# PSUM places of a recurrence given out by use, and its second state p kept at another scale

## The chip, the cores and the metric

The kernel runs on one core of a Trainium2 chip. Its engines are TensorE (PE in the profile; PEld is its weight load), VectorE (DVE), ScalarE (ACT), GpSimd (POOL) and SyncE (SP, which issues DMAs). The metric is the device time of one execution in microseconds (us). Times before are the median of three runs; the profile is of one execution.

## The reference

The input `x` has 128 sequences of 32 steps with 256 features; `cond` is one vector of 256 for each sequence. Two layers follow each other, and each adds its result to `x`.

Layer 0 runs a recurrence over the 32 steps for all 128 sequences, with states q and p that both begin as `cond`. A step is one fourth-order Runge-Kutta step (h = 0.01) of

```
dq = q - q**3 / 3 - p + x[:, t] + tanh(q) @ coupling.T + bias
dp = 0.08 * (q + 0.7 - 0.8 * p)
```

and then clips q and p to +-20. The states q of all steps go through a gated feed-forward net, 256 to 1024 to 256, whose activations and weights are quantized in blocks of 32.

Layer 1 normalizes, scales and shifts by `cond`, runs attention with 16 heads over the 32 steps of a sequence, and then a feed-forward net of the same size with Hadamard rotations, 8-bit activations and ternary weights.

## The kernel before

All arithmetic of the recurrence is in float32 tiles of 128 partitions by 256 columns. q, its stage values q2, q3 and m4, and their tanh are kept with the 256 features as two chunks of 128 partitions and the 128 sequences as columns in each chunk.

**Phase one** has the recurrence, `step(t, q, p, d)`, and behind it, for each t, the first feed-forward net and the way to the second layer's normalized input, `ffn0(t, q)`. **Phase two** has the second layer in 32 tiles of 128 tokens, `tokens(g)`. Most PSUM tiles of phase one are given up before phase two begins.

**One step.** A stage of Runge-Kutta has `slope(i, qi)`: ACT's tanh (L890) and square (L891, into PSUM); PE's coupling matmuls (L897), which add onto the stage's PSUM tile `ps[i]`; and DVE's cube (L904), which multiplies square plus constant by the stage value. DVE's `nest` (L831), a multiply and add, then makes the next stage value from `ps[i]` and the cube. So the four stages are one chain: nest, tanh, matmuls, nest. Its end is the clipped sum `add_sat` (L949) that gives the next q.

p is held negated and shifted, and z, the p of the next step, is built in p's own place by three nests and an `add_sat` (also L949). In a step p is read

- by ACT (L907), which copies it into `ps[0]` as the start of the first stage's sum;
- by DVE, in the nests that start `ps[1]`, x and z;
- by ACT (L915), which writes `part`, p at the scale of w. POOL (L917) adds q to it to give w, which ACT later brings into `ps[3]` (L933).

x is a partial sum that DVE makes early in the step and reads for `ps[2]`.

**PSUM.** A bank holds 512 float32 columns, so two places of 256. The tiles named `ps_sum` are two banks with four places. Three of them, `ps_sum` 0, 1 and 2, are one pool for z/p, x and the squares: whichever is free is taken. The fourth, `shared`, lies beside place 2 and holds small constants and scratch of the quantization: `floor`, `none` and `power` (single columns that DVE reads as bounds in the clips, L1242, and in the block scales, L993 and L1000) and `ps_tiny`. `ps[0]` and `ps[2]` are one bank (`ps_stage0`), `ps[1]` and `ps[3]` another.

**Order.** Every piece of work is recorded by `add(engine, cost, fn, reads, writes, ...)`. `Work.order` puts the pieces of each phase on the engines one by one: it keeps for each engine the earliest start, from estimated costs, dependences and free places, and breaks ties by a due time for each piece. The due times are the two strings of `TIMES`, two characters for each piece. Before a longer planned gap on PE, `keep_warm` puts matmuls of zeros (L1717). The engines then run their instructions in that order, each with waits on semaphores.

The planner knows, of PSUM banks, that a DVE instruction after DVE's own write to the same bank starts later. It has no term for two engines on one bank.

Of the kernel before, what the change touches and what calls it, by code (L numbers as in the profile page):

```python
# [25 lines left out]
ALPHA = 0.7  # L26
# [79 lines left out]
class Work:  # L106
# [15 lines left out]
            "4s6R5d4Q4A3T5X4f6d656I5v6T6B5o1_003P360_3i2A474y5l3N2L473a535E4B4n7M6E6X7i7J6m7w9IArBy5y6g6j6s6b5x84"  # L122
            "6A8w95B8CMBs6a5W745s6p6d8oAUB7BwB6C6CB9d736U9a9e7c8iBRCNCBCrEMC_AO7s8p9t9K9BAYCKC6DOEGEkFfAg8G8qAhAV"
            "9EBsCiDZEFEjEnFH7I7uAY82Em6J8s7s8Y8r9NH78c8x8P7A8H9bAS9SAw808W878c8G8G9b8mBwAZCIBK5H6u74686K4b6j2V5u"
            "3G6M736F2l4y4k5A5O6R6s7h5x6K5D5V6f5t738K6A8I7c7n706p6-647t8m8j795x7P7n8W979j97AcAUA-BBCIE9CxDpEzD2DE"
            "CaEpE9EcF2FRF8FcFjFQF_GAGJ6gGkGsGXGjGWGfGpH8GdHNHGHUHEJ07o5x6-8Q7_7Y8Y7k7d80816T84AJ7t7D7W809t7o7d9R"
            "7C7r8a9M8L8h9hAI9A999b9K8kAfAP9r8c949WAgAt9W9vAkAvBZC7CuD6E9DBFTFnCYExDSEqFVFyG5G4FsGMGHGBGVGaGgHQHK"
            "HiHbJaHfHUI4HpHXIVIQJJJJKvA87V7wANAg9TBe9cB5C68Z9W9WAG9q9EAVBOApAA9sC89fB8AhBWBnA7C9BmBSAkAZAUAWBgBP"
            "A5BCBYAs7jBhB4BsBEBaBRC2DVDYFbDrG4GeD8FJE9F5FbG7G_H9HFHuHmGzHdHYJPIUIvIuIxKSIrJ0J9J6IyJkJUMXN2OhCpA5"
            "CXB9BSBYAkBPBYCvBCBDBmBvBHCiCECTBMBpBxBaAVBzCbCeC3BxCVD8C6C4BuCNBzCgCxCXBZCQC67zDgChCPCLD4CeDeCQELGK"  # L130
            "EwHVI2FvFVFkFTGoHEIEIFHbITIdI8IyIZK5JSJpJ_K3L3JuKTKBKfJuKpLgM-OiRfBDC1CmDrBcB-D4CMDNDbEDCDDGDGCMCADO"
            "DZDwCUCaClBvClCtDCCbCaDGDyD4CPDKCCBcDRDmCRDBDFD78ND8CMDyDtGIGxH1GtIBI1HhIeIhI1IPHuIEHzIoJ0J9J1JVJUJU"
            "JkK2KxLjLZLiMQMZMFMIMbN2MqLhN5OpQbTME9DGECEVC_CoCVDSDcEFEBCwDfECDeDtDYDeDsE4DbDXDaDWDfDwE1E3DvETDyE0"
            "E8DyEKEOE9EQEUE5ETJBF9G-H7IEICIRI0JiJ2J0J2JdJrJEJPJDJLK3J-K9KrMCLHMMMALbLjOGNSMFLzNDQpN5MLNwLmN9MmOg"
            "PRQQQqEuDSDvETEbF5F8EyEcEnExFAEeEuFNFSF4F4FPFbFWFXFbFjFKFPFOFxFLFSFnFiFzFuFzFgFmF-G6G6GFJoI7J7JEJGJQ"
            "JNJRKbLbM5MeNAN9LRKJLsMHMhLsMcM5NcMZMuN4M-M_RKOuOFN4OaR0OWNaOUOePCOqPAQEQUReELEaEzFlG1GLGTGdF-G1GIGU"
            "FnG8GlGaGGGHGtGsGmGyGuGtGeGgH5H6GmGgHBHHHMH0HCH7HBHKHZHPHgKvIPJHJiJzK1KIMINwMFMSMwNQNCMTMuOZO5N-NbN1"
            "NSNHNVNLMzOKNGUGPpOfPQQdR2PwPvRCPNQTQ7QrRUSNS8G1FtGCH9HZHyH-H-HOHSHxI0HAHeI9I9HkHpI8IIIEIKIJIMHsIBIC"
            "IbIGIGIaIhIdILIiISIaIjIsInI-POJoJxMVMWOENBNaPENoObPOP6OKOTOgPCPmOQPWP9PdPFP3PQPyPSQjS7QZQYQRRmQSSIQA"
            "RzPQRnRGSVTLUZT4GqHSHcIWIrJ6I_J5IwImJCJAIcJ6JFJNJAJJJnJdJRJeJSJqJcJhJyJ-JkJnK2K7KCJvJ-K7KBKIKDK3K9No"  # L140
            "NZNIOQNuONNqN2T8P6PSQ7PxQMOyPiQgQNOXQIQrQUQ3QbQtPVQmPaQkSURBT1SyR_TMPrUMQxTsSlUKUUUvTMIvIfJ6K8KvKYLQ"
            "LDK-L8KlKkKiLoL0LELzMIKwLcLvLaLpLiLtL_LpLnLiMPLkL_LWM9M0MLMeLRMEL-M1QCPIP-PeP2O_PSPjQzQnR5RFRsS2QhRZ"
            "RkSmPkSSRgS5QoSpRKRQSeRMSIUdTgTMUdRBUUTvVCSgUdUaVcVxW2UeKjKxMhMPLmMKLzL_MSMcL_MHLoMJMgMkNFNOMHMRMLMl"
            "MNMgNqNcNGNDNvNxN7NRNCMCMpOEOUNVNQN4NMTEQYQIQdQzQuR7Q9RISwT8TYStSuT9TKUJUcT7TESUTFTfUPSxTVTjT9RLUPUq"
            "V5WPUOVsVyWEV_WAX4XHXQYWWmNDMQNhO4NKNkNoNlO2OnNmNHOaNUO7NIOiOuNoNRNqO3NxOZOeOfNnNvPGOvOGOHOUNmOZOiP3"
            "OjP4OZOXQoRRQ-RrRvSJSZRnSEU0UHVDUYUGU_UxVJVoVYUPUZUJWjVYWsVYVNVQTRVhWJXBXhWjWxWMY1YoXtY4XtY-YsYxRVNy"
            "ObPRO4PEP5P5PCPQNyOWPQPsO_PePePkOaPQPYPGP9PqQFQJP8PnQKQQPYPgPpPTQ3QMQoPrPTPQQBRaTMU1TSTDTdTeUJUGVFVO"
            "V3VqW4VgVjW8WRX8W0WcVtXrWPXfYcW7XfVrXlYJYSY8a2XqYXZ2avYSZPZGaubkc8RTQ1PxQNPpPmPnQ7QMQqPvQBQYO2QgQLQ_"
            "RFQZQrQEQZR5QYRdRcR2RFRtSLRPRcRAQwRmRFRqRqR3QmRUTDTMTeTfT2UBUXSxT1WDXCWqWpWwW6W9XmWkZBXWYJXvXyXwZLYQ"
            "XpaHZ4ZkYjYmZVbRZWXLZrYKZvZVaHbKcUcxQhQfQ-S8RKRaS4R_S4S7RgRWSKPkRyRiSNSQS8RQRYSISHSETUTXSKRsTqTiSYSO"  # L150
            "SRSlSiTUT_T0S1SYSTU6U-UZVHU-V6VGWNVsXRXsYhZ9YVYLYqXfXuZZYPYeZ2YQYZXzaAZDYycPaFZpaVaHc3auaib9bma7ahay"
            "e5d8fBRbRoSSTaRoSaTKSUTbTtTHSXUNRRTESKTsUhTCTQTNTLSwSWUNUgU8TWVEUkTGSlUGTXTQVBVCTzTlTLUhU3W4W8VyX8Wp"
            "WgYlYMYCZUZ0bCZIYza9a5YUXiZwZpZgY8aAYfZbaGb3bXb_c3bNbgbvbEbXbudUbXcvcIeseXexRwTxTsUeU8TnUsToUjU7UVTv"
            "VcUBUQTtVkVeV4UyU7VLU9UyVLWMUZUvVvVPV9W9VhV1VqWKWtVSV2VEWCYEYTXcXXXwXhYSY_YdZhamZaaOb2aTb9aHaCZfaoaM"
            "ataab1dCahc8dDdVcUcpddcaeod8dldSeidYeYeRfQfKdvR-V8VmW0UWVrVrV-W5WUVdVmWbXLVBW3W6WBW7VhVtWJVlVuVhXRW-"
            "WQWMXdVsWxX1WbXNVzVwWrWJXJWzbfaaavZha_a9aRamcRanaxbmbyc2bKc7cFb_e4cycJcod0dadJdldSdseeelfLeJekfFfwed"
            "f5fgewfsf3gwgAibSGVrWrWqXLWyXqWyXBXFX2XLXDYoXSWoXLXOZ8XxXvXCXUXoXdXjXSYoY8YSY3YOYzYgYAXNXnYlXbXwXtbh"
            "bJbAarb4aqb9eLducedkcydOd7dWd9dMd9eKdkeUd-die4fUcleCfRf3fiewfEfOgcfVg4fqfdf9gFghhzhmi8VmWLXdYGYRXwYJ"
            "YPYEYTXiYUX-XFYiZaZiZ4Y-Z7YOYvYQYCYGZ7ZeZYZKZLa5Z8YrYKYcZea2YmZ2YRZkdhb3bbcUcUcgcCeMd7e7ewdpfRfWeaf3"
            "ejfwfgfHfDfGgZf1g1fIgLfrfjgagUhAhZh5hWiShLiGgmiIinjIiSl6ZQXAYZZWZMZxa2a1ZbZzZ9Z-ZXZ8ZyZ5ZjaUaDZMaoZQ"  # L160
            "ZYZLaFaOZwa6ambDZmZ_alaHanaTapaBaaZzbTbbcXdddDcedIdMeGeTf-gOfcfpgQgNgbg4fMfxgthCgei2f-hch4hEhzifili2"
            "hOiSjhiTh9iHhCi_jkipkejol4Z9a1aBbNaEanb9b9a_b1aibEamcRakbQb4bIbmbDbOcAc8c4bObocGcQbpcEc8cicccObTbdbj"
            "dMczcHc9e9eYedeGfCeef9eif6gihZg7h7hhgMhJgChGiYgqh1h6hzhPiYi1hkiZjyikkBkNjQk8jVj9jmkbjwkjkQnlodpFbpaj"
            "bDcWd3ccdEcvbhcQcYd9cFcpcmcscUcxc-c_dCd_crdldEdJe5dteBdceEeJeie1e1dvePeGeSdSefgDh5g3ffftgIg9hFh1hQjE"
            "hNiPiui9hxhyiCiqioijixh_jQiqj9jAiDkzkikvkEkdo5kZjokUkbkol3lCpspbs8cWcCcOdoeYedeae5eHeef1eaeieAeceJe3"
            "eyf3e_egf2fdfPeNfGenf0f6fIf2fhfcebeTfGfZfcfEeufUhthVhNhAhLh8hVjBi2iJkfizjZjqjzk7iUijj0kikzkdjulNjkkO"
            "l3lfnZlbl-mjmOn4lOl0mwkJmBminYpns9uDdXemf4esfYffgMf0fYfGevfZeYf4fSgCfefhgWflfygEftgAfNgPgDgNgJgkh1gw"
            "h7g5gUglgqhLgbgEg8j4iEhZiNhpjViQhplOkfknjwlHkVk-kfkgkmk7khlblojflml4jvlslapZneoEnnoeoYomnAofmboRo5of"
            "pyrfqOesfTg1geg_gxhtgegYh4hEgdhBhChGhHhdhqhZgjh6i4gigohviQhuhPiAiEhPhihshFhliBiDiphah2gwkpjgitibi-j7"
            "jnj2mJltlwlHlKlml1lRlBlPk7lcmBm3l4lkn7lrmalhnlpGp3pEpbpNpPnqpAoMovpDq4rYsEtBgfh0hhi4i-h_j1hjiAiBj3hX"  # L170
            "h_i_hUhqhxi9jjiTi4jei1iJi5i7k9jbiziwjjjokBifi_ipirjyjOj5jlm6j3jnkSkYknklkPmblRn1lenUnemmlym5mOmDnJnL"
            "ncnRodnBnZohn8oypzqbpXpcrDpmqQqsqPpep4rVqbtIh-iPipiqjyjIkCjyjqjfkDl4j1jDkPkYjkk2kUk5kPk3kAkukMkWkikH"
            "kOkWkokZkyjfknknkUlCk_kzkwnQkSl6lDksl8lJltosmen5nLnXnvmVnbn6oHmdnnoKoSoSp4oOoRp6ozpbpLr9pyrYvIr8tXsC"
            "sdtItFs4totwjyjRkaktkdkakqknktktljkQk_kPkbkUkal4lRl0kslglKlNlpm5mFlaltm9mFlZmflZmgmNmWmemQm7nKnaoEnC"
            "n1nBnJm-mZoQnhojo9oSotocoQoTp5nGp7ompqoGpgptpfq6rCrCrFq_rGqvyJpXv0sXsbqRsXsZynrxl2krl3mrmzminJn9nHnJ"
            "mln6n5knnInSnonqnJnOnanvnHnPoAoJo7nVoLoSoFnxntnpnTngoYnjoSo2okq8ouoGnxoDoaoOnhpOpLpMpKqZpQpppJpGq0qa"
            "qgr6qirXq5rFrrpavbpFqqstrJr3uWqwumsisyqVzn-2xJpgp0oAoSodofoSoOoLoAobnloXoAofp0pAoaolodpToOoypOoqoqog"
            "qFo_p8p9paotpApjpHpvp7pRoQpXovq5qIpcqFpTqQpfrJpLq0r1tlr4qAshrou7rTr9qevZsvttvEu0qtuytauvoVqMrOoKxsoa"
            "rjqWtbpWdGf2exf4fXiYi8hfiTjElqi_kAmbe_gBkIjPjclhmZmamKmgoonsounnkMlJosoJoMpEqepfq3qHqVpuqcrHvTtsub"
        ),  # L180
        (
            "001D0n120I0d1S1i241x250M1b230w2P2e2a1_2k3E2x503V6y4x5L5f4V09605X8q4y6w5D926eAP977r7Q709I88929L8d8b9b"
# [360 lines left out]
def kernel(  # L543
# [284 lines left out]
    def nest(dst, in0, scalar, in1, rank, op1=ADD):  # L828
# [4 lines left out]
    b_p = Buf(ps_sum)  # L833
    add(
        DVE, 0.335,
        lambda: nc.vector.tensor_scalar(b_p.ap, condT, -ALPHA / BETA, -1.0, ADD, MULT),
        [b_condT], [b_p], rank=FIRST,
    )

# [940 lines left out]
```

## Time and profile before

| | |
|---|---|
| median of 3 runs | 783.18 us (782.08 to 783.4) |
| profiled execution, its own time | 783.18 us |
| its span, first to last instruction | 781.4 us |
| mean granted TensorE clock | 0.998 |
| first L907 to last L907 | 9.7 to 362.2 us |
| TensorE matmuls, busy | 722.4 us, 92% |
| VectorE, busy | 682.7 us, 87% |
| ScalarE, busy | 573.5 us, 73% |
| GpSimd, busy | 539.6 us, 69% |

L with a number is a line of the kernel. A group's row has the line, engine, operation, output and input tiles without buffer numbers, shapes, count, then busy time in us and the mean of one in ns, then the idle time of the engine just before and what ended it. A timeline row has start, duration, engine, line, and in brackets idle time with its releaser. DVE and ACT overlap the end of one instruction with the start of the next, so the spacing of two DVE instructions of 128x256 is about 0.33 us, though each is shown with 0.42.

### The profile page before, as it was taken

The numbers are of one execution on the slowest core, as the hardware profiler recorded it, in microseconds if no ns is written. First come the engines' busy times: TensorE is split into PE (matmuls) and PEld (weight loads), VectorE is DVE, ScalarE is ACT, GpSimd is POOL, SyncE is SP. The second block draws the span as 40 slices with busy tenths as digits, with TensorE's granted clock in tenths as the row PEclk, the third lists the DMA queues.
The fourth block names the chain that finished last, engine by engine and source line by source line (L and its number), as shares of the span: only waits on it lengthen the run. The fifth ranks groups of instructions, "written<-read, shape, count | busy, mean of one in ns | idle before, by whom it ended". The sixth has DMA issues, their size and how long they took to land.

```text
span 781.4 us, 26049 instructions
## 1 busy us (share of the span) xinstructions
PE 722.4 (92%) x10374; PEld 557.6 (71%) x10374; DVE 682.7 (87%) x1734; ACT 573.5 (73%) x1208; POOL 539.6 (69%) x867
## 2 busy tenths in 40 slices
PE   6778999999999999899888999999999999999986
PEld 4666677887787878777555567777677767777865
DVE  6998999998999999889828999899899999988794
ACT  3446678887887888998744688877778777686954
POOL 5765988866787778777726677787787767568320
PEclk9999999999999999999999999999999999999999
DMA  8322334323333273554450112423432242233524
GB/s 251 97 52 45 55 83 95 98 67 84 84 92 78 70 169 93 143 116 81 115 112 10 29 38 61 73 68 75 81 58 65 55 87 61 53 83 74 93 57 95
DMA packets 138521, 64.43 MB, mean 82 GB/s; under 512 B 103456, under 2 KB 137376, under 8 KB 138400
## 3 DMA queue, kind: packets, MB, share of 16 engines
q1 hardware_dynamic: 138400, 62.77, 35.3%
q8 instruction: 81, 1.33, 0.7%
q14 instruction: 40, 0.33, 0.2%
HBM read 25.77 MB, written 12.85 MB: 49 GB/s over the span
## 4 chain that ended last, share of the span: by engine, by line
PE 46%; DVE 27%; ACT 14%; issue 6%; POOL 4%; DMA 2%; DVEq 0%; ACTq 0%; POOLq 0%
PE ps_two L1668 7%; PE ps_two L1626 5%; PE ps_one L1500 5%; PE ps_stage L897 4%; PE ps_one L1570 4%; PE ps_two L794 3%; PE ps_one L1540 3%; DVE ps_sum L831 3%; PE ps_one L1593 3%; DVE slim L904 3%; DVE slim L831 3%; PE ps_one L1691 3%; ACT ps_sum L891 3%; DVE tiny L1008 2%; PE ps_turn L1392 2%
## 5 line engine op out<-in xcount | busy, mean ns | idle before, releaser
L1657 POOL TENSOR_TENSOR wide<-wide 128x512 f32<-128x512 f32 x116 | 148.2, 1301 | 59.8 <-DVE wide L1657 24.1
L897 PE MATMUL ps_stage<-slim,coup 128*128 128x128 f32 x1024 | 142.5, 282 | 12.4 <-ACT slim L890 11.3
L897 PEld LDWEIGHTS ps_stage<-slim,coup 128*128 128x128 f32 x1024 | 125.6, 191 | 37.6 <-ACT slim L890 34.7
L1318 POOL TENSOR_TENSOR mid<-mid,tiny 128x512 f32<-128x512 f32 x62 | 64.1, 1048 | 23.0 <-DVE tiny L1000 20.9
L1326 POOL TENSOR_TENSOR wide_bf<-mid,tiny 128x512 bf16<-128x512 fp8e4 x62 | 64.4, 1046 | 4.7 <-DVE mid L1242 2.4
L1668 PE MATMUL ps_two<-had_ffn,wide 128*128 128x128 f32 x512 | 63.9, 278 | 1.0 <-ACT wide L1663 1.0
L1668 PEld LDWEIGHTS ps_two<-had_ffn,wide 128*128 128x128 f32 x512 | 60.4, 192 | 5.5 <-ACT wide L1663 2.1
L1500 PE MATMUL ps_one<-w_qkv_sb,xnT 128*128 128x512 f32 x128 | 60.7, 601 | 2.5 <-DVE raws L1559 1.0
L890 ACT ACTIVATE slim<-slim 128x256 f32<-128x256 f32 x96 | 39.9, 416 | 31.1 <-DVE slim L831 30.4
L1676 ACT ACTIVATE wide<-ps_two,magic,tiny 128x1024 f32<-128x1024 f32 x32 | 38.5, 1203 | 16.3 <-DVE tiny L1457 10.6
L1657 DVE TENSOR_TENSOR wide<-wide 128x512 f32<-128x512 f32 x76 | 50.4, 697 | 0.0
L904 DVE SCALAR_TENSOR_TENSOR slim<-ps_sum,slim 128x256 f32<-128x256 f32 x96 | 40.0, 417 | 8.3 <-ACT ps_stage L907 2.4
L1663 ACT COPY wide<-ps_two 128x1024 f32<-128x1024 f32 x32 | 32.3, 1010 | 20.1 <-PE ps_two L794 19.3
L1242 DVE SCALAR_TENSOR_TENSOR mid<-mid,ps_sum 128x512 fp8e4<-128x512 f32 x64 | 43.3, 678 | 3.1 <-POOL mid L1318 2.1
L891 ACT ACTIVATE ps_sum<-slim 128x256 f32<-128x256 f32 x96 | 36.7, 382 | 11.9 <-DVE ps_sum L949 3.4
L1449 DVE TENSOR_REDUCE tiny<-ps_two 128x1 f32<-128x1024 f32 x32 | 38.9, 1216 | 5.9 <-PE ps_two L1668 5.6
L1008 DVE TENSOR_REDUCE tiny<-mid 128x16 f32<-128x512 f32 x64 | 43.1, 675 | 0.2
L1297 POOL TENSOR_TENSOR mid<-mid,mid 128x512 f32<-128x512 f32 x31 | 39.4, 1273 | 3.2 <-ACT mid L1295 2.3
L1626 PEld LDWEIGHTS <-slim_bf 128*128 128x128 bf16 x256 | 23.2, 97 | 25.7 <-issue 3.2
L831 DVE SCALAR_TENSOR_TENSOR slim<-ps_stage,slim 128x256 f32<-128x256 f32 x96 | 39.9, 416 | 1.6 <-PE ps_stage L897 0.8
L1626 PE MATMUL ps_two<-w1gT,slim_bf 128*128 128x512 bf16 x128 | 38.3, 380 | 2.7 <-DMA slim_bf<-slim_bf 1.3
L1392 PE MATMUL ps_turn<-w_qkv_sb,xnT 128*128 128x256 f32 x128 | 37.4, 417 | 2.5 <-ACT v_pad L1397 1.1
(304 smaller groups left out, 2159.0 us busy)
## 6 DMA issues: line engine op xcount, KB each, us to landing
v_dram<-v_pad SPq DMA_DIRECT2D x32, 136.0 KB, 1.9
v_pad<-v_dram SPq DMA_DIRECT2D x32, 136.0 KB, 2.2
x_step<-in_x_dram SPq DMA_DIRECT2D x32, 128.0 KB, 2.4
x_add<-in_x_dram SPq DMA_DIRECT2D x32, 128.0 KB, 2.3
x_dram<-slim SPq DMA_DIRECT2D x32, 128.0 KB, 2.0
raws<-in_L_ffn_w_gate_dram SPq DMA_DIRECT2D x4, 512.0 KB, 4.6
raws<-in_L_ffn_w_up_dram SPq DMA_DIRECT2D x4, 512.0 KB, 5.1
raws<-in_L_ffn_w_down_dram SPq DMA_DIRECT2D x4, 512.0 KB, 3.2
```

The lines of the kernel that those rows point to most:

```text
L831: add(DVE, 0.335, lambda: stt(dst.ap, in0.ap, scalar, in1.ap, MULT, op1), reads, [dst], rank=rank)
L891: add(ACT, 0.31, lambda: nc.scalar.activation(sq.ap, qi.ap, AF.Square, scale=CUBES[i]), [qi], [sq], rank=rank)
L897: nc.tensor.matmul(ps[i].ap[:, sl], lhsT=coup[COUP[i]][:, c, sl], rhs=two(th.ap)[:, c, :], start=False, stop=True, skip_group_check=True,)
L904: add(DVE, 0.335, lambda: stt(cube.ap, sq.ap, own, qi.ap, ADD, MULT), [sq, qi], [cube], rank=rank)
L1008: lambda: nc.vector.tensor_reduce(dst_of(dst.ap), blocks(src_of(src.ap)), AX.X, ALU.max, apply_absolute_value=True),
L1318: lambda it=it, ks=ks, eng=eng: eng.tensor_tensor(blocks(it.ap), blocks(it.ap), spread(binv.ap[:, ks], BLOCK), MULT),
L1326: lambda b8=b8, ks=ks, sl=sl, eng=eng: eng.tensor_tensor(blocks(bq.ap[:, sl]), blocks(b8.ap), spread(bscl.ap[:, ks], BLOCK), MULT),
L1392: nc.tensor.matmul(pv.ap, lhsT=xnT[:, c, :, t], rhs=w_qkv_sb[:, c, 2 * N :], start=(c == 0), stop=(c == NC - 1))
L1500: nc.tensor.matmul(pqk.ap, lhsT=xnT_flat[:, c, tok], rhs=w_qkv_sb[:, c, : 2 * N], start=(c == 0), stop=(c == NC - 1),)
L1626: nc.tensor.matmul(pgu.ap[:, n * HALF : (n + 1) * HALF], lhsT=two(aT.ap)[:, c, :], rhs=w[:, sr, c, :], start=(c == 0), stop=(c == NC - 1),)
L1657: eng.tensor_tensor(dv[:, :, e, :], sv[:, :, 0, :], sv[:, :, 1, :], op)
L1668: nc.tensor.matmul(pfh.ap[:, sl], lhsT=iT.ap[:, sl], rhs=had_ffn, start=True, stop=True)
```

## The change

- The four places of the two `ps_sum` banks have fixed uses: z/p and `shared` in bank 0, x and the squares in bank 1, one place each.
- p is kept at the scale that w needs: its factor is LAM = |LAST[0] / LAST[1]|. Its start value, its limits in `add_sat`, R3, R4 and the scalars of the nests that read or update it carry LAM or 1/LAM.
- ACT reads p from PSUM once in a step: a copy to `part` in SBUF, at the step's start. A second ACT instruction makes `ps[0]` from `part`, with factor 1/LAM. `part` then goes to w without a further ACT instruction.
- Both strings of `TIMES` are replaced, in nearly all of their due times (2897 of 2899 and 1751 of 1760).

Lines after the diff's parts are one or two higher in the changed kernel: the copy to `part` is L909, the one to `ps[0]` L910, the square L892, the cube L905, `add_sat` L950, the clip L1243.

```
     TIMES = (
...
-    ps_sum = banks("ps_sum", N, 4)
-    shared = ps_sum.pop()
+    ps_z, ps_shared, ps_x, ps_sq = ([slot] for slot in banks("ps_sum", N, 4))
+    shared = ps_shared[0]
...
-    R2, R3, R4 = -P3[2], -END[3], -END[4]
+    LAM = abs(LAST[0] / LAST[1])
+    R2, R3, R4 = -P3[2], -END[3] * LAM, -END[4] * LAM
...
-    b_p = Buf(ps_sum)
+    b_p = Buf(ps_z)
     add(
         DVE, 0.335,
-        lambda: nc.vector.tensor_scalar(b_p.ap, condT, -ALPHA / BETA, -1.0, ADD, MULT),
+        lambda: nc.vector.tensor_scalar(b_p.ap, condT, -ALPHA / BETA, -LAM, ADD, MULT),
...
-        x, w, z = Buf(ps_sum), Buf(slim), p
+        x, w, z = Buf(ps_x), Buf(slim), p
...
-            th, sq, cube = Buf(slim), Buf(ps_sum), Buf(slim)
+            th, sq, cube = Buf(slim), Buf(ps_sq), Buf(slim)
...
-        add(ACT, 0.36, lambda: nc.scalar.activation(ps[0].ap, p.ap, AF.Copy, scale=1.0), [p], fills=[ps[0]], rank=rank)
+        part = Buf(slim)
+        add(ACT, 0.27, lambda: nc.scalar.copy(part.ap, p.ap), [p], [part], rank=rank)
+        add(ACT, 0.3, lambda: nc.scalar.mul(ps[0].ap, part.ap, 1.0 / LAM), [part], fills=[ps[0]], rank=rank)
         started.append(work.items[-1])
         inputs(0, RAW)
-        nest(ps[1], p, h / 2 * P2[0] / K[1], q, rank)
+        nest(ps[1], p, h / 2 * P2[0] / K[1] / LAM, q, rank)
         inputs(1, HALF_STEP)
-        nest(x, p, P3[0] * h / K[2], q, rank)
+        nest(x, p, P3[0] * h / K[2] / LAM, q, rank)
         cube = slope(0, q)
-        part = Buf(slim)
-        add(ACT, 0.307, lambda: nc.scalar.mul(part.ap, p.ap, -LAST[0] / LAST[1]), [p], [part], rank=rank)
-        add(
-            POOL, 0.685, lambda: nc.gpsimd.tensor_tensor(w.ap, part.ap, q.ap, ADD), [part, q], [w],
+        add(
+            POOL, 0.685, lambda: nc.gpsimd.tensor_tensor(w.ap, q.ap, part.ap, ADD if LAST[0] * LAST[1] < 0 else SUB), [part, q], [w],
             rank=rank, port=True,
         )
-        nest(z, p, -END[0] / END[1], q, rank)
+        nest(z, p, -END[0] / END[1] / LAM, q, rank)
...
-        nest(z, z, -END[2] / R2, q3, rank)
+        nest(z, z, -END[2] / R2 * LAM, q3, rank)
...
-        add_sat(z, z, m4, edge - CLAMP, edge + CLAMP)
+        add_sat(z, z, m4, (edge - CLAMP) * LAM, (edge + CLAMP) * LAM)
```

## The prediction

> **What bounds the kernel now.** I read the page first, then busy time by stretch, the answer for the tile `ps_sum`, the timeline of one step, and the groups by line and shape.
>
> ```profile
> PE 722.4 (92%) x10374; PEld 557.6 (71%) x10374; DVE 682.7 (87%) x1734; ACT 573.5 (73%) x1208; POOL 539.6 (69%) x867
> ```
> ```profile
> 100.00:200.00 100.00, 95.08 (x690) 79.82 (x690) 92.25 (x258) 81.93 (x235) 77.03 (x99) 1.00 0.36 87
> 200.00:300.00 100.00, 97.03 (x684) 78.52 (x682) 92.46 (x253) 85.25 (x239) 78.84 (x98) 1.00 0.40 99
> ...
> 450.00:750.00 300.00, 294.79 (x6609) 221.34 (x6598) 270.14 (x654) 230.14 (x325) 214.98 (x399) 1.00 0.33 68
> ```
>
> No engine is full in phase one (to about 403 us, the first L1500 matmul): PE 95 to 97, DVE 92, ACT 82 to 85 of 100 us (columns PE, PEld, DVE, ACT, POOL). In phase two PE is busy 98% and ACT 77%. The change's operations all lie in phase one, so I look for waits there.
>
> ```profile
> L891 ACT ACTIVATE ps_sum<-slim x96: 366/387/429, 17.0 to 372.4; 128x256 f32<-128x256 f32 x96
> L904 DVE SCALAR_TENSOR_TENSOR slim<-ps_sum,slim x96: 408/416/426, 17.9 to 372.9; 128x256 f32<-128x256 f32 x96
> ...
>   ACT ps_sum L891: 11.3, 30
> ...
>   DVE ps_sum L949: 5.5, 10
>   DVE slim L904: 3.5, 6
>   ACT slim L915: 3.0, 5
> ```
> The lower four rows are idle time (us, times) of whichever engine uses a `ps_sum` tile next. One step's end shows what it is:
>
> ```profile
> 201.93 0.42 DVE L949 CUSTOM_DVE_ANT_0 ps_sum<-ps_sum,slim 128x256 f32<-128x256 f32 x1
> ...
> 202.38 0.39 ACT L891 ACTIVATE ps_sum<-slim 128x256 f32<-128x256 f32 x1 [0.26 <-DVE ps_sum L949]
> ...
> 202.80 0.37 ACT L907 ACTIVATE ps_stage<-ps_sum 128x256 f32<-128x256 f32 x1
> ...
> 203.21 0.42 DVE L904 SCALAR_TENSOR_TENSOR slim<-ps_sum,slim 128x256 f32<-128x256 f32 x1 [0.60 <-ACT ps_stage L907]
> ...
> 203.66 0.38 ACT L915 ACTIVATE slim<-ps_sum 128x256 f32<-128x256 f32 x1 [0.49 <-DVE slim L904]
> ```
> The square needs only m4, yet waits for z's update (0.26). The cube needs only the square, yet waits 0.60 for ACT's read of p, and ACT's second read of p waits 0.49 for the cube. These data don't touch; they share a PSUM bank. The program's wait lists hold a wait for every such pair on two engines, read against read too. I counted them and joined them with the trace: DVE and ACT wait so on each other 176 times on the two `ps_sum` banks, and in 101 of them the engine stands, 29.5 us together. By kind: a square behind DVE's z, p, x or bounds 10.9 us; DVE behind a square it doesn't read 7.8; ACT's two reads of p against the cubes and nests, both ways, 10.9.
>
> How much of that sets the end: copies L907 run from 9.7 to 362.2 us over 31 steps, 11.37 us a step. A stage's chain is nest 0.42, tanh 0.42, matmuls 1.05, with hops of 0.03, 0.05 and 0.04: 2.0, so 8.0 a step. Issue spacing gives PE 9.7 and DVE 9.7 a step. If each stage takes the longest of 2.0 and what DVE, ACT and PE hold between its neighbours in their order, a step takes 10.49 (mean of steps 5 to 30). The trace has 10.95 there. The 0.46 between, 14.7 us over 32 steps, is what waits can add; the rest is work.
>
> **The change, part by part.** The sum is made against the profiled execution: 783.18 us, of which 781.4 is the span and 1.8 lies around it; it equals the median of the three runs.
>
> *Places.* z/p moves to bank 0 with the bounds, x to bank 1 with the squares. In the changed order 94 cross-engine bank waits remain. By the mean standing time of the like kind before: 31 squares behind a nest at 0.10 (3.18 us over 32) is 3.1; 27 nests behind a square at 0.17 (4.27 over 25) is 4.6; 31 DVE instructions behind the copy of p at 0.14 (5.25 over 37) is 4.4; 5 copies of p behind DVE at 0.43 (5.64 over 13) is 2.2. Together 14.3, so 15.2 of the 29.5 goes. Taken over steps 3 to 30, a step is 0.68 us longer for each us of such standing (correlation 0.5): 10.3 us off the path. By the other measure, 15.2/29.5 of the 14.7, it is 7.6. I take 9 and keep 0 (all beside other work) and 13 for the range. What is late next is DVE and PE content.
>
> *The new wait.* DVE's next touch of bank 0 after z's update waits for the copy of p; it is a clip (L1242) 17 times, else a scale or a nest. Behind it in DVE's queue stand cubes and the state's clipped sum, for which ACT's tanh and then PE wait. In 12 of the 30 such waits after the first step DVE reaches that instruction within 0.43 us of z, while hop and copy take 0.07+0.37. That is the 4.4 above; the cover of the others is 0.66 us or more of DVE work.
>
> *The copies.* ACT had p to PSUM and p to `part`, both from PSUM; it has p to `part`, then `part` to PSUM:
>
> ```profile
> L907 ACT ACTIVATE ps_stage<-ps_sum 128x256 f32<-128x256 f32 x32 | 12.3, 384 | 3.6 <-DVE tiny L1000 2.2 <-PE ps_stage L897 0.6 <-DVE ps_sum L836 0.6
> L915 ACT ACTIVATE slim<-ps_sum 128x256 f32<-128x256 f32 x32 | 12.2, 381 | 6.1 <-DVE slim L904 3.5 <-DVE ps_sum L949 2.1 <-DVE ps_stage L831 0.5
> L1334 ACT COPY ps_po<-x_add 128x256 f32<-128x256 f32 x31 | 11.6, 375 | 0.3
> L1346 ACT COPY slim<-ps_po 128x256 f32<-128x256 f32 x31 | 11.4, 369 | 0.3
> L1562 ACT ACT_TABLE_LOAD x13 | 16.7, 1283 | 0.2
> L1634 ACT ACT_TABLE_LOAD x13 | 16.7, 1283 | 0.5 <-PE ps_two L1626 0.3
> ```
> A copy from PSUM to SBUF is L1346 (369 ns), from SBUF to PSUM L1334 (375): 744 ns a step for 765, or 0.7 us less in 32 steps, beside other work: taken at nothing, bounds -0.7 and 0. PSUM's stage 0 gets p one copy later (about 0.4 us, or 0.9 with one other ACT instruction between), and PE's drive transposes (L865) follow it. The coupling matmuls need it only after the state's tanh, 205.95 in the step above for a copy that began at 202.80: covered by some 2 us. Without cover it would be 0.4 a step, 13 us.
> The Trainium skill (Perfetto Trace Analysis, Optimizing Scalar/DVE Operations) gives ScalarE an access overhead of about 93 ns on SBUF against 51 on PSUM. It speaks against reading `part` instead of p: an estimate from that page is 42 ns x 32 = 1.3 us more on ACT. The rows above show no such step between the two kinds of source, and they decide; by the page the sum would be 1.3 us higher if nothing covered it.
>
> *The order.* The due times are new for both phases. By the same stage by stage reckoning the changed order gives 10.61 us a step for 10.49: 0.12 x 32 = 3.8 us more (DVE 9.76 for 9.71, PE 9.83 for 9.73). DVE's instructions right behind its own write to the same bank are 17 for 9; such a pair starts 0.034 us after the end where others start 0.091 before it, so 8 x 0.125 = 1.0. Tanh stands behind a square in 18 stages for 13, inside the reckoning. In phase two ACT has four more table loads, 4 x 1.283 = 5.1 us. ACT has 70 us free in the 300 of the windows above while PE holds the pace: taken at nothing, 5.1 if that cover fails. PE has the same real work, and 92 warm-up matmuls in phase two for 93, 138 before it for 128: those fill idle time, nothing. The phase boundary keeps its sequence but not its interleaving; I bound it at 2 us either way, one more or one fewer of the PE waits seen there.
>
> *The constants* (LAM in scales, limits and bounds) change no instruction's shape: nothing. SP and GpSimd issue as many instructions; GpSimd's sum w gets `part` earlier, which can't delay it.
>
> The sum: 783.2 - 9 + 3.8 + 1.0 = 779.0.
>
> **Rivals.**
> *Nothing moves:* the bank waits stand beside work, and DVE and PE, at 9.7 of each 11.4 us, set the step. For it: a step's length follows its bank standing only loosely (0.5). Then what the order adds is also partly hidden: 783.
> *Slower, through the copy of p:* bounds and z in one bank put DVE's FFN instructions behind an ACT copy. It decides where the copy ends more than about 0.7 us after z's update, since DVE then stands in most of the 31 places instead of 12. For it: ACT is busy 85 of 100 us, so its queue is often late. At ACT's own 0.43 each it costs 13.3 instead of 4.4, so the sum becomes 779.0 + 8.9 = 788. Against it: the copy stands right behind the square of m4, which no longer waits for z.
> *More:* the order's 3.8 is absorbed, and 13 us comes off: about 771.
> That the change doesn't do what it says is partly so: x and squares keep 58 waits. They are in the sum.
>
> **How the numbers follow.** Forecast 0.45 (775 to 781.5), more 0.15 (767 to 775), nothing 0.12, slower 0.28 (784.8 to 791, the table loads included). No change means within 0.2%, 781.6 to 784.7, about what a measurement of this kernel can tell. Faster 0.60, same 0.11, slower 0.29. The range leaves out a tenth at each side: 769 to 788.5.
>
> **What would show it.** In the profile after: squares (L892 there) no longer idle for z's update (L950) or a clip, cubes not for ACT's read of p; the copies of p 11.24 us apart instead of 11.37; phase two as long as before within 3 us. I am wrong if the pitch stays while the bank waits are gone (work sets it), if clips and scales idle behind the copy of p by more than 8 us together, or if the difference lies in phase two.

## The result and the profile after

The changed kernel takes 777.73 us (median of four runs, 777.34 to 779.6) where the kernel before takes 783.29 (782.08 to 783.73). The ratio is 0.9936, with a 95% interval of 0.9916 to 0.9956: 5.6 us less. The profiled execution of after took 779.6 us, with a span of 777.8.

Page of after, busy time of each engine:

```profile
PE 724.8 (93%) x10383; PEld 557.8 (72%) x10383; DVE 688.7 (89%) x1734; ACT 574.7 (74%) x1212; POOL 538.7 (69%) x867
```
Busy time by stretch of after, with the columns of the prediction's table:

```profile
100.00:200.00 100.00, 98.50 (x706) 80.82 (x705) 96.44 (x270) 84.49 (x243) 84.62 (x105) 1.00 0.37 88
200.00:300.00 100.00, 98.05 (x700) 79.89 (x698) 93.00 (x253) 84.49 (x243) 78.51 (x99) 1.00 0.40 101
...
450.00:750.00 300.00, 294.05 (x6478) 220.11 (x6477) 273.48 (x656) 235.57 (x328) 213.96 (x392) 1.00 0.33 69
```
In the first stretch DVE gets through 270 instructions for 258 and is busy 96.44 us for 92.25. In the second it is as before (253 instructions both times), and the stretch in phase two nearly so, with ACT busy 5.4 us more.

The answer for the tile `ps_sum` of after (duration min/median/max in ns, first and last start; the lower rows are idle time, us and times, of the engine that uses the tile next):

```profile
L892 ACT ACTIVATE ps_sum<-slim x96: 363/370/405, 18.3 to 367.3; 128x256 f32<-128x256 f32 x96
L905 DVE SCALAR_TENSOR_TENSOR slim<-ps_sum,slim x96: 406/414/426, 18.7 to 367.7; 128x256 f32<-128x256 f32 x96
...
L909 ACT COPY slim<-ps_sum x32: 352/372/383, 9.5 to 354.9; 128x256 f32<-128x256 f32 x32
...
  DVE slim L832: 6.2, 7
  DVE ps_sum L950: 4.1, 5
  ACT ps_sum L892: 3.8, 16
  DVE ps_stage L832: 3.8, 5
  ACT slim L909: 2.2, 5
```
Waiting for a square (L892) fell from 11.3 us in 30 places to 3.8 in 16, and "DVE slim L904", DVE's cube, is gone from the list. "DVE slim L832" is no bank wait: that instruction makes the next stage value, which the square reads. "DVE ps_stage L832" is one: a square behind DVE's read of x, which shares its bank.

The end of one step in the timeline of after (start and duration in us, engine, line):

```profile
198.36 0.43 DVE L950 CUSTOM_DVE_ANT_0 ps_sum<-ps_sum,slim 128x256 f32<-128x256 f32 x1
198.40 0.43 ACT L891 ACTIVATE slim<-slim 128x256 f32<-128x256 f32 x1
198.72 0.39 ACT L892 ACTIVATE ps_sum<-slim 128x256 f32<-128x256 f32 x1
...
199.04 0.37 ACT L909 COPY slim<-ps_sum 128x256 f32<-128x256 f32 x1
199.14 0.42 DVE L905 SCALAR_TENSOR_TENSOR slim<-ps_sum,slim 128x256 f32<-128x256 f32 x1
...
199.52 0.69 DVE L1243 SCALAR_TENSOR_TENSOR mid<-mid,ps_sum 128x512 fp8e4<-128x512 f32 x1
199.72 0.49 ACT L910 ACTIVATE ps_stage<-slim 128x256 f32<-128x256 f32 x1
```
No brackets: nothing idles here. Square and cube run beside z's update and the copy of p, which before held them up by 0.26 and 0.60. The cube starts 0.78 us after the start of z's update; before it was 1.28.

Counted as in the prediction, 94 bank waits between DVE and ACT remain, and the engines stand 8.7 us at them for 29.5. The last coupling matmul (L898) starts at 368.0 us instead of 373.2: 5.2 us of the gain lie in the recurrence. Between the end of a stage's coupling matmuls and the start of the DVE instruction that makes the next stage value, the four stages of a step lose 1.71 us for 1.94 (means of the first 31 steps). The other parts of the chain moved by −0.05 (to tanh), +0.03 (tanh to matmuls) and +0.02 us (the matmuls) a step. Together that is 7.3 us over these steps. Of it 2.1 are given back: the first coupling matmul starts 0.7 us later, and the last step's stages take 1.4 us longer.

### The profile page after: what moved, and what is told of

Read it like the earlier page. It is cut to its first block, busy times and chain, and to the rows that moved or that the text cites. A ratio compares the mean times of both kernels' runs of the same rounds, so it can differ in the third digit from the quotient of the medians.

```text
span 777.8 us, 26076 instructions
## 1 busy us (share of the span) xinstructions
PE 724.8 (93%) x10383; PEld 557.8 (72%) x10383; DVE 688.7 (89%) x1734; ACT 574.7 (74%) x1212; POOL 538.7 (69%) x867
## 4 chain that ended last, share of the span: by engine, by line
PE 38%; DVE 15%; ACT 10%; POOL 6%; issue 4%; DMA 1%; DVEq 0%; ACTq 0%; POOLq 0%
PE ps_two L1669 6%; PE ps_two L1627 5%; PE ps_one L1501 4%; PE ps_one L1571 3%; PE ps_stage L898 3%; PE ps_one L1541 3%; PE ps_two L795 3%; PE ps_one L1594 2%; PE ps_one L1692 2%; DVE wide L1658 2%; DVE tiny L1450 2%; PE ps_turn L1393 1%; PE ps_gu L1284 1%; DVE wide L1642 1%; DMA wide_bf<-wide_bf 1%
## 5 line engine op out<-in xcount | busy, mean ns | idle before, releaser
L1658 POOL TENSOR_TENSOR wide<-wide 128x512 f32<-128x512 f32 x116 | 148.6, 1305 | 55.9 <-DVE wide L1658 21.6
L898 PE MATMUL ps_stage<-slim,coup 128*128 128x128 f32 x1024 | 143.0, 283 | 10.4 <-ACT slim L891 8.9
L898 PEld LDWEIGHTS ps_stage<-slim,coup 128*128 128x128 f32 x1024 | 125.9, 191 | 37.2 <-ACT slim L891 33.7
L1319 POOL TENSOR_TENSOR mid<-mid,tiny 128x512 f32<-128x512 f32 x62 | 64.4, 1050 | 12.5 <-DVE tiny L1001 10.5
L1501 PE MATMUL ps_one<-w_qkv_sb,xnT 128*128 128x512 f32 x128 | 61.3, 605 | 2.3 <-DVE coup L1526 0.8
L1658 DVE TENSOR_TENSOR wide<-wide 128x512 f32<-128x512 f32 x76 | 53.9, 739 | 0.5 <-POOL wide L1658 0.4
L1243 DVE SCALAR_TENSOR_TENSOR mid<-mid,ps_sum 128x512 fp8e4<-128x512 f32 x64 | 43.4, 680 | 4.7 <-ACT slim L909 2.2
L892 ACT ACTIVATE ps_sum<-slim 128x256 f32<-128x256 f32 x96 | 36.2, 377 | 10.4 <-DVE slim L832 6.2
L905 DVE SCALAR_TENSOR_TENSOR slim<-ps_sum,slim 128x256 f32<-128x256 f32 x96 | 39.9, 415 | 2.4 <-ACT ps_sum L892 1.9
L832 DVE SCALAR_TENSOR_TENSOR slim<-ps_stage,slim 128x256 f32<-128x256 f32 x96 | 39.9, 415 | 1.5 <-PE ps_stage L898 1.0
L1292 ACT ACTIVATE mid<-ps_gu 128x512 f32<-128x512 f32 x64 | 37.8, 599 | 1.9 <-PE ps_gu L1284 1.7
```

What stands on the lines that cost most here:

```text
L832: add(DVE, 0.335, lambda: stt(dst.ap, in0.ap, scalar, in1.ap, MULT, op1), reads, [dst], rank=rank)
L898: nc.tensor.matmul(ps[i].ap[:, sl], lhsT=coup[COUP[i]][:, c, sl], rhs=two(th.ap)[:, c, :], start=False, stop=True, skip_group_check=True,)
L1243: lambda: stt(dst.ap, src.ap, TOP, floor.ap.to_broadcast([P, n]), ALU.min, ALU.max, saturate=False),
L1319: lambda it=it, ks=ks, eng=eng: eng.tensor_tensor(blocks(it.ap), blocks(it.ap), spread(binv.ap[:, ks], BLOCK), MULT),
L1501: nc.tensor.matmul(pqk.ap, lhsT=xnT_flat[:, c, tok], rhs=w_qkv_sb[:, c, : 2 * N], start=(c == 0), stop=(c == NC - 1),)
L1658: eng.tensor_tensor(dv[:, :, e, :], sv[:, :, 0, :], sv[:, :, 1, :], op)
```

## The experiments

"Standing" is DVE's and ACT's idle time at bank waits on the `ps_sum` banks, up to the end of the instruction that holds the bank; "pairs" are DVE instructions right behind DVE's own write to the same bank. A is the start of the last coupling matmul and B the time from there to the last matmul, in us of the profile. "Order" is the sequence of instructions on every engine: that of before (old), of after (new), or another. Each ratio is to executions of before that were taken alongside.

| kernel | order | time, us | ratio to before, 95% | standing | pairs | A | B |
|---|---|---|---|---|---|---|---|
| before | old | 783.29 | 1 | 29.5 | 9 | 373.2 | 404.7 |
| after | new | 777.73 | 0.9936 [0.9916, 0.9956] | 8.7 | 17 | 368.0 | 406.3 |
| e12: order alone | new | 792.38 | 1.0130 [1.0087, 1.0173] | 30.7 | 42 | 381.3 | 404.5 |
| e6: order, places | new | 784.67 | 1.0019 [1.0003, 1.0036] | 19.0 | 17 | 374.3 | 406.2 |
| e11: single read alone | old | 783.15 | 0.9991 [0.9971, 1.0011] | 24.8 | 9 | 374.0 | 403.3 |
| e3: places alone | old | 787.90 | 1.0064 [1.0047, 1.0080] | 24.0 | 70 | 379.2 | 402.9 |
| e10: places, single read | old | 787.60 | 1.0044 [1.0027, 1.0060] | 20.1 | 70 | 378.4 | 403.7 |
| e2: after, squares beside z/p | new | 798.59 | 1.0202 [1.0182, 1.0222] | 40.9 | 53 | 388.6 | 404.2 |
| e2b: after, squares beside bounds | new | 777.00 | 0.9923 [0.9908, 0.9938] | 10.6 | 40 | 367.2 | 404.4 |
| e4: after, one pool | another | 808.90 | 1.0332 [1.0318, 1.0345] | 23.0 | 16 | 393.5 | 409.5 |
| e8: after, x in SBUF | new | 784.69 | 1.0019 [1.0006, 1.0032] | 2.0 | 17 | 373.4 | 403.7 |
| e9: after, x and z/p in SBUF | new | 834.42 | 1.0658 [1.0645, 1.0672] | 0.0 | 4 | 425.9 | 403.3 |
| e1: after, phase two's old due times | new in phase one | 778.97 | 0.9954 [0.9936, 0.9973] | 8.5 | 17 | 368.5 | 405.6 |
| e5: before, phase two's new due times | old in phase one | 786.29 | 1.0024 [1.0008, 1.0039] | 29.5 | 9 | 373.4 | 407.4 |

**Are the bank waits on the path? Squares beside z/p (e2).** The changed kernel, its order kept: after the planner has run, the squares' place and the bounds' place are exchanged.

```
     issue = work.order()
+    for slots_, k in ((ps_x, 2), (ps_sq, 1)):
+        slots_[0].ap = place[k]
     ... bounds and scratch: place[3] for place[1]
```


> The changed kernel with every engine's order unchanged; only addresses move: squares beside z/p, bounds beside x. DVE and ACT then have 183 waits on each other that only a bank explains, instead of 94, and 53 instead of 17 DVE instructions come right behind DVE's own write to their bank. Theory (the standing at bank waits makes the phase): standing of about 30 us instead of 8.7, of which half is on the path (10), and 36 x 0.125 = 4.5 from the own-bank pairs, mostly on the path: 790 us (785 to 794), all of it in phase one. Rival (the gain came from the new order, the bank waits stand beside work): the own-bank pairs alone, 778 to 782.

It took 798.59 us. The standing went up by 32.2 us and A by 20.6, more than was expected. Two rows of its tile answer for `ps_sum`, and three of its timeline:

```profile
  ACT ps_sum L893: 14.7, 43
  DVE ps_sum L833: 11.4, 22
```
```profile
211.42 0.42 DVE L906 SCALAR_TENSOR_TENSOR slim<-ps_sum,slim 128x256 f32<-128x256 f32 x1 [0.78 <-ACT slim L910]
...
213.75 0.39 ACT L893 ACTIVATE ps_sum<-states 128x256 f32<-128x256 f32 x1 [0.52 <-DVE ps_sum L833]
214.17 0.43 DVE L833 SCALAR_TENSOR_TENSOR ps_stage<-ps_sum,states 128x256 f32<-128x256 f32 x1 [0.45 <-ACT ps_sum L893]
```
Here the cube (L906) again waits for the copy of p (L910), a square for a nest, and the next nest for that square: the same order and data, another bank. The order has 36 more pairs as well, but at the 0.125 us of the prediction they are 4.5 us, and the next run shows 23 more of them at no cost. So these waits set the end, in this order. The rival that they stand beside work, 778 to 782, falls.

**The other bank for the squares (e2b).** As e2, but x goes beside z/p and the squares beside the bounds:

```
+    for slots_, k in ((ps_x, 1), (ps_sq, 3)):
+        slots_[0].ap = place[k]
     ... bounds and scratch: place[2] for place[1]
```


> The changed kernel with every engine's order unchanged; x beside z/p, squares beside the bounds. Bank waits 124, of them 88 between squares and DVE's clips and scales of the net, 31 of nests behind the copy of p; own-bank pairs 40. Theory (any pairing but the changed one costs, by the same line): standing 15 to 25 us and 5 us of pairs, phase one 5 to 10 us longer, 783 to 788 us. Rival (squares and bounds meet seldom, so this pairing is as good): 777 to 780.

777.00 us, standing 10.6: as good as the changed kernel, whose interval its own overlaps, so the rival held. What pays is that the squares lie away from z/p. Its 23 more pairs show no cost: A is even 0.8 earlier.

**The order with neither part (e12).** After's order, but `ps[0]` is made from p in PSUM again, and x and the squares take in turn whichever of two places is free, one beside z/p and one beside the bounds.

```
+    free, given = [1, 2], {}
+    for item in issue:
+        for b in item.bufs:
+            if b in last and b not in given:
+                given[b] = free.pop(0)
+        free += [given[b] for b in item.bufs if last.get(b) is item]
...
-        add(ACT, 0.3, lambda: nc.scalar.mul(ps[0].ap, part.ap, 1.0 / LAM), ...
+        add(ACT, 0.3, lambda: nc.scalar.mul(ps[0].ap, p.ap, 1.0 / LAM), ...
```


> The changed kernel's order on every engine, with neither of the two parts: p is read from PSUM twice, and x and the squares take in turn whichever of two places is free, one beside z/p and one beside the bounds. Theory: the changed order is no gain by itself; over three kernels in that order the last coupling matmul comes 0.56 us later for each us that DVE and ACT stand at bank waits, so with the standing of before (about 30 us, more if the turn falls badly) it comes at 379 to 384 for 373.2 before, and the time is 788 to 793. Rival: the order is at least as good as the old one whatever the places, and most of the gain is its own: 777 to 783, with the last coupling matmul at 373 or earlier.

792.38 us, A at 381.3: the theory held. The new order alone, with 42 pairs for 9, is 1.3% slower than before, at about before's standing (30.7). Two rows of its groups by line and shape (count, then busy us and mean ns, then idle time before and its releasers):

```profile
L906 DVE SCALAR_TENSOR_TENSOR slim<-ps_sum,slim 128x256 f32<-128x256 f32 x96 | 40.3, 420 | 9.3 <-ACT slim L910 4.0 <-ACT ps_sum L893 2.3 <-ACT ps_stage L911 1.1
L910 ACT COPY slim<-ps_sum 128x256 f32<-128x256 f32 x32 | 11.9, 370 | 8.5 <-DVE slim L906 7.4 <-DVE ps_sum L951 0.7 <-DVE ps_sum L838 0.2
```
The copy of p (L910) waits 7.4 us for cubes, and cubes 4.0 for it. In after the cubes idle 2.4 and no copy waits for a cube.

**Places without the single read (e6).** Only the source of `ps[0]` is undone; the order is kept.

```
-        add(ACT, 0.3, lambda: nc.scalar.mul(ps[0].ap, part.ap, 1.0 / LAM), [part], fills=[ps[0]], rank=rank)
+        add(ACT, 0.3, lambda: nc.scalar.mul(ps[0].ap, p.ap, 1.0 / LAM), [part], fills=[ps[0]], rank=rank)
```


> The changed kernel in the same order, but the copy to the first stage's PSUM reads p from PSUM instead of part from SBUF, so ACT reads p from PSUM twice a step as before; bank waits 122 instead of 94. Theory (the single read is a small part of the gain): 28 more waits at 0.09 us, the mean standing of the changed kernel, is 2.5 us, half of it on the path: 779 us (778 to 781). Rival (the single read is most of the gain, because DVE then stands behind a late second read): 782 or more. Rival (it is worth nothing): 777.7.

784.67 us, A 6.3 later than after, standing 10.3 more: the rival that the single read matters held. The row of the second read in its groups by line and shape, and then the same instruction in after:

```profile
L910 ACT ACTIVATE ps_stage<-ps_sum 128x256 f32<-128x256 f32 x32 | 12.0, 376 | 5.7 <-DVE mid L1243 3.4 <-DVE slim L1243 0.7 <-DVE tiny L1001 0.6
```
```profile
L910 ACT ACTIVATE ps_stage<-slim 128x256 f32<-128x256 f32 x32 | 12.8, 401 | 0.4
```
With bounds and z/p in one bank, the second read waits 4.1 us for clips (L1243), and DVE's clips and scales idle 4.3 behind it. Read from `part`, it idles 0.4. So e12, e6 and after split the change, in one order: places −7.0 us of A (381.3 to 374.3), single read −6.3 more (to 368.0). Together 13.3 us for 22.0 us less standing, 0.60 for each. The places also take away 25 pairs; the single read leaves them at 17 and gives 6.3 us for 10.3 less standing, 0.61 for each, so the rate does not hang on the pairs.

**The parts in the old order (e3, e11, e10).** Before's order exactly; after the planner has run, places are given by use (e3), or `part` and `ps[0]` are both made where p's first read stood, with two SBUF tiles of its own for `part` (e11), or both (e10).

```
 e3, e10:
+    for use, k in (("z", 0), ("x", 2), ("sq", 3)):
+        for b in by_use[use]:
+            b.slots, b.slot = [Slot(place[k])], 0
     ... bounds and scratch: place[1]
 e11, e10:
+        def p_once():
+            nc.scalar.mul(part.ap, p.ap, c_part)
+            nc.scalar.mul(ps[0].ap, part.ap, 1.0 / c_part)
-        add(ACT, 0.36, lambda: nc.scalar.activation(ps[0].ap, p.ap, AF.Copy, scale=1.0), [p], fills=[ps[0]], rank=rank)
+        add(ACT, 0.36, p_once, [p], fills=[ps[0]], rank=rank)
```


> The kernel before with every engine's order unchanged and p read twice as before; only addresses move: z/p beside the bounds, x beside the squares. Bank waits between DVE and ACT 122 instead of 176, but DVE instructions right behind DVE's own write to their bank 70 instead of 9, since the order was made for the old places. Theory (bank waits count, own-bank pairs count at 0.125 each): standing about 17 us instead of 29.5, -6 us on the path; +7.6 us for the pairs, some 5 of it on the path: 782 us (778 to 785), the places alone bring little without an order made for them. Rival (places alone are the whole change): 777 to 778. Rival (neither counts): 783.3.

> The kernel before with p read once: at the place of ACT's first read it writes part (SBUF tiles of its own) and then PSUM from part; the later read of p is gone. Old places, old due times, every other instruction where it was. Bank waits 160 instead of 176. Theory (a second ACT read of p in the middle of the step costs the path, whatever the order): the later read's standing of 6.5 us goes, 0.56 of it on the path, and DVE's nest of z no longer waits for it: 779 us (777 to 781). Rival (it costs only in the new order, where DVE is fuller): 783. Rival (the first stage's PSUM, now one copy later, becomes late): 785 or more.

> Both parts of the change, places by use and p read once, in the order of the kernel before; 106 bank waits, 70 own-bank pairs. Theory (the two parts belong together, and own-bank pairs cost 0.12 to 0.19 each): from the 787.9 of the places alone, some 11 us less standing at the two reads of p, 0.56 of it: 782 us (779 to 784); the new order is needed for the rest. Rival (the parts alone carry the gain, the order is none of it): 777 to 778. Rival (the old order under the new places is the loss itself): 786 or more.

787.90, 783.15 and 787.60 us. The theories of a gain fell: in the old order neither part gains, and the places lose 4 to 5 us. In e11 the rival that the single read costs only in the new order held (783), in e10 the one that the old order under new places is the loss (786 or more); e3 is slower than any of its three forecasts. In e3 ACT's first read of p meets clips, as in e6 (groups by line and shape):

```profile
L912 ACT ACTIVATE ps_stage<-ps_sum 128x256 f32<-128x256 f32 x32 | 12.0, 374 | 7.9 <-DVE mid L1247 3.0 <-DVE slim L1247 2.0 <-PE ps_stage L902 1.0
```
e10 has this read from `part`, 9.4 us less standing than before, and is still slower. It has 61 more pairs; at the prediction's 0.125 us they are 7.6 us of DVE time, enough for A's 5.2. But 23 more pairs were free in e2b, so this is possible and not shown. What is shown: in the old order the edits gain nothing, in the order that came with them they do.

**One pool again (e4).** The places go back to the rotating pool and the planner runs anew, with after's due times.

```
-    ps_z, ps_shared, ps_x, ps_sq = ([slot] for slot in banks("ps_sum", N, 4))
-    shared = ps_shared[0]
+    ps_sum = banks("ps_sum", N, 4)
+    shared = ps_sum.pop()
     ... and Buf(ps_sum) for z, x and the squares
```


> The changed kernel with the places undone: z/p, x and squares take turns in one pool of three places as before, bounds in the fourth; single read of p and the due times as in the changed kernel (the planner puts a few instructions elsewhere). Bank waits between DVE and ACT 151 instead of 94, own-bank pairs 16. From the first runs, all in the changed order: phase one ends 0.56 us later for each us of standing at bank waits plus 0.125 for each own-bank pair (10.8 us: 368.0; 21.1: 374.3; 47.5: 388.6). Theory (this line holds): with 151 waits at 0.1 to 0.2 us the standing is 15 to 30 us, phase one 2.5 to 12 us longer, time 781 to 789 us, and the measured standing puts its own point on the line within 2 us. Rival (the places matter only where squares lie beside z): 778 to 780.

808.90 us: a miss as an undo. With other places free at other times the planner made another order, with 10431 matmul records for 10383 (48 more warm-ups). Its standing, 14.3 above after's, is some 9 us at 0.61 for each; A is 25.5 later, so the line that was expected fails by some 17 us. That rest came with the other order and has no run of its own. e12 asks the same question with the order held.

**No bank at all (e8, e9).** x (e8), and z/p too (e9), in SBUF tiles of their own, order kept.

```
+    own_x = tile_of("own_x", [P, N])
+    ps_x[0].ap = own_x
     ... e9 also: own_z for ps_z
```


> The changed kernel, same order, but x lies in a tile of its own in SBUF, so the squares have their bank alone. Bank waits 37 instead of 94 (those with the copy of p). Theory (the line): 6.8 us less standing, 3.8 us off, 774 us (773 to 776). Rival (the nest that reads x then has two SBUF inputs, as GpSimd's instructions have, and either is slowed): GpSimd's or DVE's rows longer, 778 to 782.

> The changed kernel, same order, with x and z/p both in SBUF tiles of their own: no bank wait between DVE and ACT is left on these two banks, and no own-bank pair of z. Theory (the line): 8.7 us less standing and 2 us less of pairs, 0.56 of it, 6 us off: 772 us (770 to 775). Rival (two SBUF inputs in eight more DVE instructions of a step slow DVE or GpSimd): some 8 x 0.1 us a step or more, 780 us or above, with longer rows of L832 or of GpSimd's multiplies.

784.69 and 834.42 us, with 2.0 and 0.0 us of standing: both slower than after, so both theories fell. The rivals' longer rows are there, in e8 with a time above their 778 to 782. Groups by line and shape of after, of e8 and of e9, for DVE's multiply-and-add instructions:

```profile
L832 DVE SCALAR_TENSOR_TENSOR ps_stage<-ps_sum,slim 128x256 f32<-128x256 f32 x32 | 13.6, 425 | 1.2 <-ACT ps_sum L892 0.9
```
```profile
L833 DVE SCALAR_TENSOR_TENSOR ps_stage<-own_x,slim 128x256 f32<-128x256 f32 x32 | 24.1, 753 | 0.0
```
```profile
L834 DVE SCALAR_TENSOR_TENSOR own_z<-own_z,slim 128x256 f32<-128x256 f32 x64 | 39.4, 616 | 0.1
L834 DVE SCALAR_TENSOR_TENSOR own_x<-own_z,states 128x256 f32<-128x256 f32 x31 | 29.4, 949 | 0.3
L834 DVE SCALAR_TENSOR_TENSOR ps_stage<-own_z,states 128x256 f32<-128x256 f32 x31 | 27.3, 882 | 0.0
```
With one input in PSUM and one in SBUF the instruction takes 425 ns; with both in SBUF 616 to 949. In the timeline of e8, beside GpSimd:

```profile
77.31 2.34 POOL L1060 TENSOR_TENSOR wide<-wide,wide 128x1024 f32<-128x1024 f32 x1 [1.09 <-DVE wide L1058]
77.48 2.46 DVE L833 SCALAR_TENSOR_TENSOR ps_stage<-own_x,slim 128x256 f32<-128x256 f32 x1
```
DVE's instruction begins 0.17 us after GpSimd's and ends 0.29 after GpSimd's end (79.94 for 79.65). The Trainium skill (SBUF — State Buffer, Who interferes with whom) says that a VectorE instruction with two SBUF inputs and a GpSimd instruction that reads SBUF contend, and that the later of the two is blocked until the other is done; these rows agree. Of the 32 instructions of this row in e8, 27 began while a GpSimd instruction ran, and 25 of these ended 0.29 us after it; the five that met none took 420 to 424 ns. Two SBUF inputs alone cost nothing here; meeting GpSimd does. So the SBUF copy of x removes 6.7 us of standing and adds 10.5 us of DVE time (24.1 for 13.6), and A comes 5.4 later.

**Phase two's due times (e1, e5).** The changed kernel with before's second string of `TIMES`, and before with after's.

```
 e1:  TIMES = (after's first, before's second)
 e5:  TIMES = (before's first, after's second)
```


> The changed kernel with the due times of phase two as before; phase one is instruction for instruction that of the changed kernel, and ACT has 28 table loads again instead of 32. Theory (phase one gained some 6.8 us and the new order of phase two gave back 3.3 of it): the last coupling matmul and the first L1501 matmul at 368 and 396.4 us as in the changed kernel, phase two 374.6 us as before, time 774.4 us (773 to 776). Rival (phase two is longer because of the state in which the new phase one leaves it, not because of its order): phase two stays at 377.9, time 777.7.

> The kernel before with the new due times of phase two alone; phase one unchanged, ACT has 32 table loads instead of 28. Theory (the order of phase two is worth nothing, as the changed kernel with the old one showed): 783.3 (782 to 785). Rival (the new order lengthens phase two, by the 3.3 us seen between the two profiles or by the 5.1 us of table loads): 786 to 788.

e1 took 778.97 us, e5 786.29. The rival held in both. With the new phase one, phase two's old due times gain nothing, and the table loads, 28 for 32, don't show. With the old phase one the new ones cost 0.2% [0.1%, 0.4%]. So phase two's due times are not the source of the gain.

**B and the clock.** B is 402.9 to 404.7 us in the eight profiles with a full granted clock from there on, in either order, and 404.2 to 409.5 in the six with a dip in it. Windows of after around the change of phase (the last three columns are granted clock, DMA share, GB/s):

```profile
370.00:380.00 10.00, 7.55 (x53) 5.04 (x52) 8.27 (x19) 6.01 (x16) 8.91 (x12) 1.00 0.43 97
380.00:390.00 10.00, 8.73 (x43) 6.49 (x44) 4.63 (x9) 4.29 (x12) 0.74 (x2) 0.83 0.45 110
...
420.00:430.00 10.00, 8.82 (x307) 6.21 (x298) 8.17 (x19) 2.48 (x5) 4.71 (x20) 0.83 0.07 18
```
The mean of 0.83 over 10 us is 3.4 us at half clock, twice in this execution and not in before's. In the 3.4 us just ahead of the two, PE was busy 1.75 us (378.50 to 381.90) and 2.22 us (419.50 to 422.90). The other executions of after had spans of 775.5, 776.3 and 775.5. In the new order four profiles with a full clock from A on (e12, e2b, e8, e9) have a B of 403.3 to 404.5, no more than before's. So the 1.6 us of B, and with it the profiled time above the median, likely go with the dips and not with the change; how much each costs wasn't isolated, and e5's B of 407.4 with one dip stays unexplained. Ahead of A, the profiles of e3, e5, e6, e8, e10, e11 and e12 have one such dip and e9's has several, where those of before and after have none. In e5, which has before's phase one, it is one at 39.4 us, and A comes 0.2 us later.

## Why the prediction was right, point by point

- **Bank waits are on the path: right, and larger.** The sum had 15.2 us of standing gone and 9 off the path, 0.59 for each. At a fixed order 22.0 went for 13.3, 0.60 for each. The rate was right; the remaining standing was the mis-sized term, 8.7 for 14.3. By kind: squares behind a nest 4.96 (3.1 foreseen), nests behind a square 1.87 (4.6), DVE behind the copy of p 0.94 (4.4), the copy behind DVE 0.97 (2.2). Of the 4.96, 2.3 are one wait in the first step, where the stage value that the square reads is ready only 0.50 us before the square starts; the other squares stand 2.7, about as foreseen. For the other three kinds the prices per wait from before's order were too high: the new order puts these instructions where the wait is mostly over.
- **The room for waits: misread, on the low side.** The prediction has 10.95 us for a step of the trace (steps 5 to 30). From coupling matmul to coupling matmul, and from copy of p to copy of p, it is 11.1, so over its 10.49 there is room for some 20 us of waits instead of 14.7. The lower of its two measures then gives some 10 us off the path instead of 7.6, beside the 10.3 of the other. The 9 was a choice between the two; that its 0.59 for each us comes so near to the measured rate is partly luck.
- **The new wait behind the copy of p: real and cheap.** Priced at 4.4, measured 0.94; the profile's own row has clips idle 2.2 us behind L909, against a bound of 8. In after 7 of 17 clips stand. The slower rival needed the copy late after z's update; in the step above it starts 0.25 us after z's end, because the square ahead of it no longer waits. But e6 shows that this rival was one edit away: with two reads of p, clips and reads hold each other up and the gain is gone.
- **The order's cost: too low.** Predicted 3.8 + 1.0. e12 against before, at nearly equal standing, has A 8.1 us later, of which 1.2 us more standing explains 0.7. That leaves 7.4, but e12's own places also have 33 more pairs than before where the change has 8 more. After against before, with 8 more pairs alone, gives nearly the same: 20.8 us less standing at 0.61 are 12.7, and A came only 5.2 earlier, so the order cost some 7.5 us by this estimate. The stage by stage reckoning missed 2.7 of it. The two errors, 12.7 for 9 and 7.5 for 4.8, partly cancelled: −5.2 by A where the sum had −4.2. That the total came out so near is luck.
- **Parts that add up: not so.** The sum treated places, single read and order as terms. In the old order places and single read together are +0.4%, in the new one −1.9% (0.9936 against 1.0130). No term is a property of the edit alone.
- **Copies at nothing: right.** L910 from SBUF has a mean of 401 ns, not the 375 of the row it was taken from, and from PSUM in e6 376: 25 ns, or 0.8 us in 32 steps (10 ns by the medians, 388 and 378). The Trainium skill (Perfetto Trace Analysis, Optimizing Scalar/DVE Operations) gives ScalarE an overhead of about 93 ns on SBUF and 51 on PSUM; the direction agrees with these rows, the difference of 42 ns is more than they show. PE's drive transposes idle 10.6 us behind the second copy, for 6.0 behind the first before; the chain of stages shows none of it, so the cover of some 2 us held.
- **Phase two unchanged within 3 us: just missed by the prediction's mark, right by B.** From the first L1501 matmul, at 396.4 for 403.3, it is 377.9 for 374.6, 0.3 outside. But that mark itself moved 1.7 us nearer to the last coupling matmul; from A the rest is 1.6 longer, with the two dips.
- **Signs in the profile.** Of the ones named, the squares' idle time for z's update and the cubes' for the read of p are gone, as said. The copies are 345.4/31 = 11.14 us apart, for 11.24 foreseen and 11.37 before; that is 7.1 us less over 31 steps, of which A shows 5.2.

Open: why the places alone lose in the old order (pairs are one candidate), why the last step is longer in the new one, and what of B belongs to the dips. The new order with the old places and the single read was not run.

## What to carry to other kernels

Where two engines use one PSUM bank, list the pairs that meet by time, not by data: the tile that an engine off the chain reads at the chain's end (here p) should not share its bank with the tiles that the chain writes and reads at that time (here the squares). What else lay beside p, the bounds (777.73 us) or x (777.00), made no difference. In the old order this change was worth nothing, or less; measure edit and order crossed (four kernels), not the edit added to the old order. And before moving a tile to SBUF to be free of banks, see whether DVE then reads two SBUF inputs beside a busy GpSimd.

## What was not expected of the hardware

- DVE's multiply and add of 128x256 float32 went from 425 ns to means of 616 to 949 once both inputs were in SBUF beside GpSimd's tensor operations, up to 2.57 us for one. In e8 those that met no GpSimd instruction took 420 to 424.
- The granted TensorE clock fell to half for about 3.4 us near the change of phase in the profiled execution of after, and not at all in another (mean clock 1.0, span 775.5 us). PE was busy 7.55 of the 10 us from 370 to 380, but only 1.75 of the 3.4 just ahead of the dip.
- Exchanging x and the squares between the two banks, with instructions and order untouched, is worth 21.6 us (e2 against e2b).
